# Adding the masked values of the two parities on VectorE before TensorE sums the heads, with a rewritten order of instructions

## The chip, the cores and the metric

The kernel runs on one core of a Trainium2 chip. The core has five engines, each with its own instruction queue: PE (TensorE, matrix multiplication, with a separate queue entry PEld for loading the stationary operand), DVE (VectorE), ACT (ScalarE), POOL (GpSimd) and SP (SyncE, which here only issues DMA transfers). Matmuls write to PSUM, which has eight banks; everything else works on SBUF. The metric is the device time of one execution in microseconds, as the median of several. The kernel before takes 224.31 us (three runs, 224.06 to 224.98).

## The reference, cut to what matters

Two rows (t = 0 and 1) of 128 tokens with 512 channels pass three residual blocks: a self-attention with a cross-attention over 2048 context tokens and a feed-forward part, an RWKV block, and a "switch head" attention. The change lies in the last, and reorders all of them. The last block has 8 heads of 64 channels and 5 experts; each head chooses 2 of 5 experts for its values and 2 of 5 for its output:

```python
q = (x @ Wq).reshape(b, t, h, dh).transpose(0, 2, 1, 3)
k = (x @ Wk).reshape(b, t, h, dh).transpose(0, 2, 1, 3)
gl_v = (x @ Ws).reshape(b, t, h, e)
wv = _topk_mask(gl_v, SEL) * jax.nn.sigmoid(gl_v)
xv = jnp.einsum('btd,edk->btek', x, Wv)
v = jnp.einsum('bthe,btek->bhtk', wv, xv)
probs = jax.nn.softmax(jnp.einsum('bhid,bhjd->bhij', q * scale, k), axis=-1)
attn = jnp.einsum('bhij,bhjd->bihd', probs, v)
gl_o = (x @ Wd).reshape(b, t, h, e)
mask_o = _topk_mask(gl_o, SEL)
out = jnp.einsum('bthe,bthk,ekd->btd', mask_o, attn, Wo)
```

The last line is what the change touches: for every token, the attention output of a head (64 values) is multiplied by the 0/1 mask of its 5 experts, the products of the 8 heads are summed to 5 x 64 = 320 values, and these go through a 320 x 512 projection.

## The kernel before, in words

All work is written down first and issued afterwards. The calls on the engines are recorded in a list (`Engine`, L172 to L182), one entry per instruction, 1759 in all, and `Program.emit` (L166) issues them in the sequence that the string `ORDER` (L42 to L99) gives, a list of entry numbers written out by hand. The order of the instructions on every engine, SP's DMA queue included, follows from that string. Since all are issued from one line, nearly all rows of the profile carry L169, and the tiles' names tell them apart.

The phases are, for both rows: queries and self-attention, `cross_queries`, `cross_attention`, `feed_forward`, `rwkv`, `switch_heads`. In the order they overlap: while row 0 is in one phase, row 1 is in the same or the one before. Four resources tie them together:

- Weights for matrix products that run as two halves (high and low part, fp32r) are loaded in pieces of 128 x 512 into a tag of three buffers (`stage`, L330); ACT casts each piece to its high half and DVE subtracts to get the low half. A load on SP waits until the piece three before it has been subtracted, and holds all loads behind it in SP's queue. In the profile these are the casts and subtractions `hl_Wv<-w_Wv`, `hl_fc2`, `hl_Wk` and so on.
- Context pieces (1 MB; `cT` for the scores, `cN` for the values) are loaded into 16 buffers of 8 KB a partition (`wide`, L201), shared with whole weights such as fc1, Wa, Wg, Wf, and with `me` and `ve` in the last phase. They are cast and subtracted in the same manner (`hl_ctxT`, `hl_ctxN`).
- The eight banks of PSUM (`bank`, L198).
- Tiles of 128 x 512 (`row`, L207).

In the cross-attention the number of context tokens that count is found from the scores (`em`, `left`, a small matmul with `nones`, `nsb` on ACT, then `some` and the masked exponentials). In the feed-forward part fc1 gives `zf` and its halves `zTh`. In `rwkv`, DVE forms K, the norms and decay products (`kn`, `kk`, `pr`, `kkar`, `kr`, `rn`, `wd`), then `Y` for each row, which PE turns and multiplies by Wo; `spread` tiles hold parameter rows, among them LNFB, which is added to the residual `X` in place.

`switch_heads` (L999): `xn` is turned to `xnT`; `w_fcat` gives the gates and the experts' values, `w_fWq` and `w_fWk` give queries and keys. DVE finds the top two experts by comparing all pairs (`gt`, `eq`, `ahead`, `sel`), and `v` from five products `ve`. Heads are taken by parity: heads 0, 2, 4, 6 share one PSUM bank for the scores (`nb`, `es`, `eT` for the softmax) and one for the attention output, heads 1, 3, 5, 7 the others. `ri` is the reciprocal of the softmax's sums, `mo` the output mask times `ri`. For each parity, `me` holds 4 heads x 5 experts x 64 masked values.

The two rows end differently. Row 0 adds all its masked values on DVE and turns the sum. Row 1 leaves the sum over the heads to PE: a matmul of a 128-wide piece of `me` (two experts) with the identity matrix `unit` turns the piece and accumulates in PSUM, so that 8 matmuls (4 heads, 2 parities) give one of three 128-row chunks of the turned sum `aT`; ACT copies it out, and `w_fWo` is applied. The three chunks start at experts 0, 2 and 3; the third overlaps the second by one expert, whose rows in the third chunk of `w_fWo` are zero. For row 1 the second parity's products are made in pieces of two, two and one experts (`pairs`), the first parity's in one instruction.

`keep_warm` issues matmuls of `unit` with itself; four of them are given for the first chunk of row 1's end, and the order places them well before it.

Of the kernel before, what the change touches and what calls it, by code (L numbers as in the profile page):

```python
# [42 lines left out]
0 208 1 209+1 215 2 1698 216+1 1718 218 1719 219+1 1699 232 221 1700 8 4 211 3 212 233 222 25 234 20 235+1 214 213 238  # L43
237 228 223+1 26 239 229 21+1 31 244+1 225 246 1720 270 240 247 27 230+1 241 271+3 248 275+2 249 28 34 37 226 23+1
278+1 250+5 280 242 227 256 281 257 243 258+2 282+1 261+3 284+1 265+1 286 29 292 30 32 293+1 287+2 267 35 318 33 295+2
319+1 38 298 36 299+1 321 39 301 322 302+2 323+4 305 328+1 306+1 330+1 5 308+1 332 310+4 333+2 315 40+1 49 43+1 11 19
336 9 337+2 290 268+1 317 340+1 344+1 414 316 415 45 42 346+1 375 12 50 79 46+1 84 376 66 48 291 343 358+1 342 360 377
361 416 51 362 378 348 363 18 379 417 364 87 67 63 418 104 380 419 349 381 365 384 382 56 420 423 350+4 395 366 383
385+1 85 387+2 421+1 424 390 425 69 426 391 6 355 367+1 392 357 396 356 427 393 428 369 429 68 434 371 370 372 397 394
398+3 430 402 373 431+1 435 404+1 433 57 403 436+2 406 1721 407+3 1701 453 463 411 454 10 80 439 455 464 456 465 457  # L50
441 443 466 440 442 447 467 444 468 82 458+2 448 469 74 445 86 88 446 473 483 474 470 450 449 475+2 484+2 478+2 58 64
60+1 471 81 461 481 487+2 493 94 59 62 89 494 490 495+1 462 482 521+2 497 491 65 75 472 524 492 498 525+2 499 528 500
529 109 83 530 501+4 531 97 126 532 374 506 533 77 76 534 507+6 535+1 95 514+2 537+2 98 540 517 541+1 588+1 562 96 518
543+1 563 72 575 564 576 545 78 519 590+2 577 593 565+6 594 578 546 579 70 73 572 549 573 580+1 550 582+1 71 551+2 105
584+1 99 547 106 520 548 92+1 554 586 555+1 595 90 727 596 557 91 558+2 597+1 728 157 599 107 729 102 100 574 108 587
121 127 561 730+2 600 112 733+1 129 735 601+3 101 736+1 618 740+5 738 605 611 606 612 609 746+1 753 748+1 610 607+1
613 54 766+1 754+1 750+1 768+1 615 614 756+2 641 770 623+3 642 771 122 759 103 760 55 643 761 772 616 627 128 773+1
762 775+2 130 644 739 628 123 629 617 630+4 124 635 125 645 137 136 138 763+1 646 752 765 928 636 659 778 660+2 637
140 638+2 779 131 142 663+1 780 647+4 132+1 652+2 781 113+1 134 782 655+1 796 168 657+1 665+1 677 667 135 668 785 783
678 669+2 679 672 787 680 13 15 110 786 784 673+2 789 681 790 676 682+1 619 684 788 791 145 197 792 17 14 794 52 837+2  # L60
7 840 801+1 795 855 803 53 169 139 793 804+1 685 819+1 807 821 856 822 808 857 141 16 111 146 806 809+2 686 812+1 118
143 687 823 814 688 815 689 816+1 692 818 144 825+1 693 824 827+1 858 147 158+1 690 696 829 697 691 830 698+1 831 700
832+2 701 835 841+1 412 115+1 694 702 119 703 413 120 695 117 704+1 150 620 152 706 836 148+1 621 187 622 859 188 151
843+1 707 710 708 711 709 712 845+3 713 163+1 178 849+1 179 714 797 715 451 851+1 165 189 853+1 860+1 716 720+1 153
862 717 723 722 718 180 719 863 904 864 725 905+1 916 866 917 867 907+2 452 865 870+1 868 874 910 875+2 911 170 981
724 869 872 878 154 879 155 880+2 918 160 166 873 883+2 919 161 920+1 913 912 156 914 726 922+1 929+1 798+2 175 931
176 924 167 932 925 162 926 915 933 172 888 886 934+2 889 887 890+2 937 177 938 184 927 893 939+1 894+1 898 199 943
941 896+1 944 942 899+1 969 957 901 173 970 945 958+4 185 963+1 946 966 947+1 971+1 951 949 952 965 950 953+1 973+2
967 955 976+1 956 982 968 983+2 193 902 978 986 1010 987 1011 979 988 1013+1 989+1 1012 991 980 992 1015 1089 1016 993
1017 1099 174 186 181 903 994 1090 996 1020 1067 1022 1069 1108 1018 1107 997 995 998 1091 1024 1140 1092 1073 1109  # L70
1026 1071 1141+1 1139 1028 1100 1029 1075 1093+1 1076 198 1077 1095 1030+1 1101 1070 1021 190 1096 1023 1032 1078 999
182 1033 1102 1116+1 1068 1079 1034 1080 191 196 1001 1004 1000 1025 1005 1035 1002 1006 1003 1007 183 1008 1103 1027
1009 1036 171 1072 1218+1 1081 1037 1221 194 1038 1082 1220 1222 1224+1 1039 1223 1097 195 192 1111 1110 1228 1324
1083 1112+2 1118 1323 1327 1119 1226 1229 1325 1333 1328 1084 1334+1 1326 1085 1336 1045 1329 1040 1074 1086 1343 1231
1279 1098 1282 1307 1346 1330 1280 1308 1232 1281 1233 1283 1046 1305 1344 1230 1234 1044 1306 1115 1047 1284 1286+2
1042+1 1104 1285 1019 1289 1337 1290 1347 1291+1 1235 1293+1 1120 1105 1087 1041 1048 1352 1295 1088 1296 1345 1391
1353 1297 1354+1 1348 1148+1 1392 200 1054 1389 1349+1 1106 1390 1050+1 1309 1150+1 201 1052 1331 1049 1121 1123 1236
1055 1061 1338 1124 1393 1299 1298 1300 1053 1060 1125 1310 1332 1311+1 1237 1122 1356 1339 1127 1238+3 1131 1242+1
1058 1244+1 1301 1341 1059 1246+2 1143 1340 1056 1062 1132 1351 1144 1128 1064 1342 1133 1063 1065 1302 1129 1357 1130
1303 1399 1145+1 1135 1057 1126 1313 1066 1314 1152 1359 1315 1253 1136 1254 1360 1137 1376 1358 1400 1316+3 1256 1252  # L80
1249 204 1250 1170 1401 1134 1251 1255 1138 1153 1257 1264 1258+1 1377 1261 1154 1361 1265 1155 1304 1147 1156 1158+1
1263 1320 1157 1161+1 1164 202 1369 1262 1260 1268 1321 1160 1165 1171 1166 1163 1167 1172 1168 1363 1378 1173+1 1276
1402 1198 1190 1394 1322 1277 1395 207 1373 1278 1379 1273 1267 1270 1269 1374 1380 1382 1362 1272 1371 1375 1274 1169
1396 1364 1271 203 1366 1275 1175 1381 1176 1383 1177 1384 1372 1385+2 1365 1178 1367+1 1388 1180 1179 1370 1266
1181+2 1397 1184 1186 1185 1187+1 1199+2 1189 1202 1191+1 205 1193+1 1403 1398 1203 1404 1406 1405 1407+2 1204 1410+1
1205 1424 1415 1195 1412+2 1416 1418 1417 1419+2 1196+1 1206+3 1212 206 1210 1213 1211 1214+3 1473 1425 1452 1426+2
1422 1472 1475+1 1444 1474 1423 1478+1 1429+2 1477 1481 1480 1432 1487 1482 1434 1433 1436 1435 1227 1437 1483 1440+1
1484 1438+1 1442 1488 1445 1485 1446 1489 1522 1453+2 1523 1447 1443 1513 1456 1448 1511 1486 1457 1524+1 1505 1526+1
1514+1 1490 1516 1496+1 1491+1 1517 1528 1518 1529 1493+1 1498 1519 1499 1520 1506+4 1500 1449 1521 1495 1530 1501
1512 1531 1502+2 1559 1534 1458 1450 1459 1451 1460+3 1466 1464 1467 1465 1468+2 1533 1471 1560+2 1602 1601 1603 1532  # L90
1604 1607+1 1563 1605 1539+2 1606 1567 1542 1564 1536 1610 1609 1543 1565 1611 1566 1535 1612+1 1569 1545 1544 1547
1546 1570 1552 1642 1549 1643 1572+1 1550 1614 1571 1551 1651 1553+1 1652 1537+1 1653 1555 1575 1556 1576 1574 1577
1548 1616 1654 1557+1 1617 1635 1634 1636+1 1568 1644+1 1618+1 1578 1646+1 1620+1 1648 1615 1625 1655 1622 1656 1623
1649 1638 1657 1640 1582 1650 1658 1624 1626+4 1639 1631 1659 1632 1688+1 1633 1579 1641 1663+1 1580 1583 1581 1690+1
1584 1660 1585 1662 1668+2 1586 1692 1671 1696 1587 1661 1588+1 1695 1672 1590 1705 1676 1706 1596 1591 1597 1673+1
1678 1675 1681 1679 1682 1665 1694 1592 1666 1693 1702 1667 1703 1680 1684+1 1683 1686 1677 1712 1687 1707 1697 1704
1708 1713 1709+2 1714 1716+1 1715 1598 1593 1731+1 1722 1733 1740+1 1734 1594 1599 1735 1600 1742 1723+4 1736+1 1743
1728+1 1738 1744+1 1730 1749 1746 1739 1747+1 1595 1754 1750+3 1755+3
"""  # L99
OPT = set("""psc fc2 Wv Wk u2col bfpe z4pe z1pe q2 hhcol q2row d3 both1 both4""".split())  # L100

ON_ACT = [set("vsum vc vv bv".split()), set("vsum vc vv bv".split())]
PCR = [{0,1,2},{0,1,2}]
WHOLE = set("Wv1 Wv2 fc2 Wv Wk".split())
VPE = set()
MIX = {"Wq1": 2}
MIXD = set("Ww Wa Wr".split())
CUTW = 2
# [77 lines left out]
def perceiver_kernel(ctx: ExitStack, tc: tile.TileContext, a: dict, out: bass.AP):  # L186
# [46 lines left out]
    for t in range(T):  # L233
        for j in range(2):
            sync.dma_start(X[t][:, half(j)], a["x"][t][:, half(j)])
# [296 lines left out]
    def token(t):  # L532
        return slice(t * P, (t + 1) * P)
# [678 lines left out]
```

## Time and profile before

| What | us |
|---|---|
| median of three runs | 224.31 |
| profiled execution, whole | 224.74 |
| its span in the profile | 222.9 |
| PE busy | 215.3 (97%) |
| DVE busy | 186.1 (83%) |
| ACT busy | 140.2 (63%) |
| last matmuls of the gates for row 1 (`w_fcat`) start | 189.90 |
| first matmul of row 1 with `v` starts | 208.56 |
| first sum of row 1's masked values starts | 211.29 |
| last addition (`res`) starts | 219.47 |

A line of the timeline gives the start, the duration, the engine, the line, the operation, the tiles (result first), their shapes and the count of equal instructions in a row; in brackets stands how long the engine had been idle before it and what ended the wait. The granted clock of TensorE was 0.998 of full speed. A matrix product in plain f32 shows as two records for each matmul. PE's records overlap, so the distance between starts is the cost of one, and not its duration. The span is 1.8 us shorter than the whole profiled execution, which is 0.43 us above the median.

### The profile page before, as it was taken

To read this page: it belongs to the slowest core of one execution; us is meant where nothing else is said; L and a number is where in the kernel's file an instruction comes from. 1 tells how busy PE (TensorE), PEld (TensorE's weight loads), DVE (VectorE), ACT (ScalarE), POOL (GpSimd) and SP (SyncE) were. 2 spreads that over 40 slices of the span, in tenths; PEclk is the share of its full clock that TensorE was granted. 3 is DMA by queue.
4 is the path that set the end of the run, shared out by engine and by line. 5 is a ranking of instruction groups with operands and counts; after the bars stand their busy time and mean duration, and the time that the engine had idled before them with its cause. 6 is when DMAs were issued, how large, how long until landed. Compare 5 with 4: busy or idle time off the path is not lost.

```text
span 222.9 us, 3686 instructions
## 1 busy us (share of the span) xinstructions
PE 215.3 (97%) x1246; PEld 182.7 (82%) x1246; DVE 186.1 (83%) x439; ACT 140.2 (63%) x400; POOL 17.1 (8%) x40
## 2 busy tenths in 40 slices
PE   6999999999999999999999999999999999998993
PEld 6999879998778767868788888887886799797892
DVE  4670569998999998989989999999998598999831
ACT  2753569686788998827469889977652614705500
POOL 4200011000000000000111100021213001000000
PEclk9999999999999999999999999999999999999999
DMA  6987799926699999587854999900000000000011
GB/s 157 355 322 255 250 381 386 385 110 238 245 315 354 374 399 375 202 285 209 310 187 102 402 389 387 303 7 0 3 0 0 0 3 1 0 3 0 0 50 47
DMA packets 21897, 43.42 MB, mean 195 GB/s; under 512 B 1283, under 2 KB 2871, under 8 KB 21879
## 3 DMA queue, kind: packets, MB, share of 16 engines
q1 hardware_dynamic: 21879, 43.19, 55.1%
q8 instruction: 10, 0.16, 0.3%
q14 instruction: 8, 0.07, 0.1%
HBM read 42.66 MB, written 0.52 MB: 194 GB/s over the span
## 4 chain that ended last, share of the span: by engine, by line
PE 64%; DVE 24%; DMA 3%; issue 2%; POOL 2%; ACT 2%; SPq 0%; POOLq 0%; DVEq 0%
PE bank L169 64%; DMA w_Wv<-in_Wv_dram 3%; DVE me L169 2%; DVE hl_ctxT L169 2%; DVE Y L169 2%; DVE pr L169 2%; DVE st L169 1%; DVE em L169 1%; DVE hl_ctxN L169 1%; POOL rinv L169 1%; POOL rs L169 1%; DVE ve L169 1%; DVE v L169 1%; DVE u L169 1%; DVE hl_Wv L169 1%
## 5 line engine op out<-in xcount | busy, mean ns | idle before, releaser
L169 POOL TENSOR_TENSOR rinv<-ve,nhalf 128x1 f32<-128x1 f32 x16 | 10.1, 629 | 147.2 <-DVE ve L169 75.4
L169 DVE TENSOR_TENSOR hl_ctxT<-cT,hl_ctxT 128x1024 fp32r<-128x1024 f32 x16 | 19.0, 1216 | 0.8 <-ACT hl_ctxT L169 0.5
L169 PE MATMUL bank<-hl_ctxT,qkTh 128*128 128x512 f32 x64 | 17.8, 395 | 0.1
L169 ACT CAST hl_ctxT<-cT 128x1024 fp32r<-128x1024 f32 x16 | 16.0, 1050 | 2.5 <-PE bank L169 2.5
L169 PE MATMUL bank<-hl_ctxN,pTh 128*128 128x512 f32 x48 | 16.3, 402 | 0.0
L169 DVE TENSOR_TENSOR hl_ctxN<-cN,hl_ctxN 128x1024 fp32r<-128x1024 f32 x12 | 14.4, 1217 | 0.6 <-ACT hl_ctxN L169 0.6
L169 PEld LDWEIGHTS bank<-hl_ctxT,qkTh 128*128 128x128 f32 x64 | 11.7, 188 | 2.8 <-DVE some L169 0.5
L169 DVE TENSOR_TENSOR hl_Wv<-w_Wv,hl_Wv 128x512 fp32r<-128x512 f32 x12 | 8.0, 681 | 6.4 <-ACT hl_Wv L169 6.4
L169 ACT CAST hl_ctxN<-cN 128x1024 fp32r<-128x1024 f32 x12 | 12.3, 1046 | 0.0
L169 PE MATMUL bank<-hl_ctxT,qkTl 128*128 128x512 f32 x32 | 10.4, 396 | 0.0
L169 PEld LDWEIGHTS bank<-hl_ctxN,pTh 128*128 128x128 f32 x48 | 8.9, 189 | 1.6
L169 PE MATMUL bank<-xnT,w_fWk 128*128 128x128 f32 x64 | 10.2, 276 | 0.0
L169 PE MATMUL bank<-hl_ctxN,pTl 128*128 128x512 f32 x24 | 10.1, 421 | 0.0
L169 ACT CAST hl_Wv<-w_Wv 128x512 fp32r<-128x512 f32 x12 | 7.3, 622 | 4.0 <-DMA w_Wv<-in_Wv_dram 3.9
L169 PE MATMUL bank<-xnT,w_fWq 128*128 128x128 f32 x64 | 9.9, 277 | 0.0
L169 PEld LDWEIGHTS bank<-u2T,w_fc 128*128 128x128 f32 x64 | 8.2, 191 | 1.4 <-ACT u2T L169 1.1
L169 PEld LDWEIGHTS bank<-xnT,w_fWq 128*128 128x128 f32 x64 | 8.6, 192 | 0.7 <-ACT xnT L169 0.3
L169 PEld LDWEIGHTS bank<-xnT,w_fWk 128*128 128x128 f32 x64 | 8.9, 192 | 0.2
L169 PE MATMUL bank<-u2T,w_fc 128*128 128x128 f32 x64 | 8.5, 278 | 0.3 <-ACT u2T L169 0.3
L169 PE MATMUL bank<-w_Wa,mix 128*128 128x256 f32 x32 | 8.7, 379 | 0.0
L169 PE MATMUL bank<-unit 128*128 128x128 f32 x32 | 6.9, 391 | 1.7 <-POOL unit masks.py:199 1.7
L169 PE MATMUL bank<-w_Wr,mix 128*128 128x256 f32 x32 | 8.4, 379 | 0.0
(289 smaller groups left out, 614.8 us busy)
## 6 DMA issues: line engine op xcount, KB each, us to landing
cT<-in_ctxT_dram SPq DMA_DIRECT2D x8, 1024.0 KB, 6.7
cN<-in_ctx_dram SPq DMA_DIRECT2D x8, 1024.0 KB, 7.5
spread<-in_spread_dram SPq DMA_DIRECT2D x9, 512.0 KB, 8.5
w_Wv<-in_Wv_dram SPq DMA_DIRECT2D x12, 256.0 KB, 5.3
w_Wk<-in_Wk_dram SPq DMA_DIRECT2D x8, 256.0 KB, 5.3
w_Wq<-in_Wq_dram SPq DMA_DIRECT2D x4, 256.0 KB, 4.5
w_Wk2T<-in_Wk2T_dram SPq DMA_DIRECT2D x4, 256.0 KB, 6.9
w_Wq<-in_Wq_dram SPq DMA_DIRECT2D x1, 1024.0 KB
```

Of the source, the lines that this page charges most:

```text
L169: self.tc.keep_in_program_order(op(*args, **kwargs))
```

## The change

In `switch_heads`, for row 1 and before the sums of each chunk, DVE adds the second parity's masked values to the first's, for the experts of that chunk's pair (two, two, one). The chunk is then summed by four matmuls, not eight. In numbers of recorded calls: three DVE additions more (4 heads x 2, 2 and 1 experts x 64), twelve f32 matmuls of 128 x 128 fewer. Loads, ACT's and POOL's work are the same sets as before.

`ORDER` is rewritten as a whole: 1750 instructions of the changed program in a new sequence on all engines, SP's loads included. The diff also adds code for options that are not switched on (`xact`, `pow1`, `u1back`), and takes out an unused one (`veps`); none of these changes an instruction.

```diff
-OPT = set("""psc fc2 Wv Wk u2col bfpe z4pe z1pe q2 hhcol q2row d3 both1 both4""".split())
+OPT = set("""psc me2 fc2 Wv Wk u2col bfpe z4pe z1pe q2 hhcol q2row d3 both1 both4""".split())
...
             for c, e in enumerate((0, 2, 3)):
                 pt = bank([P, P])
                 keep_warm(0 if c else TAILW[2], pt)
-                matmuls(pt, [(m[:, i, e : e + 2, :].rearrange("p e d -> p (e d)"), unit) for m in me for i in range(4)], True)
+                if "me2" in OPT:
+                    n = pairs[c]
+                    dve.tensor_add(me[0][:, :, n], me[0][:, :, n], me[1][:, :, n])
+                ms = me[:1] if "me2" in OPT else me
+                matmuls(pt, [(m[:, i, e : e + 2, :].rearrange("p e d -> p (e d)"), unit) for m in ms for i in range(4)], True)
                 act.copy(aT[:, c, :], pt)
```

Parts of the new order that the prediction speaks of, told by what is issued on each engine:

- End of row 1, DVE: both reciprocals and both `mo`, the odd parity's products of the pairs 2-3 and 0-1, the even parity's product, the additions for 2-3 and 0-1, the odd product of the last expert, the last addition. Before: the even product first, then the three odd ones. PE: the odd parity's matmuls with `v` first, then all six matmuls of row 0's `w_fWo`, the twelve sums (chunks at 2, 0, 3), six matmuls of row 1's `w_fWo`. Before, four of row 0's six stood ahead of the matmuls with `v`, and one of row 1's six between the sums.
- `rwkv`: the addition of LNFB to row 1's X, the reduction `kkar` and the first half of `wd` that stood behind row 0's Y now stand ahead of it; the reduction `kr` of row 1 and `rn` now stand behind.
- Feed-forward: no cast of a weight stands between ACT's `zf` activations of row 0.
- Loads on SP: a `cT` piece ahead of two pieces of Wv1; one piece of Wv2 right behind the pieces of Wk2T; the first `cN` piece behind three `cT` pieces; fc1 behind a second fc2 piece and a pair of `spread` rows; Wa behind fc1; fWk, Wr, Wo, Wg, Ww in this sequence; Wf last.
- POOL: the iota for `kidx` after two of the first reciprocal roots; the clearing of `w_fWo`'s last rows ahead of most of the later roots.

## The prediction

> **What bounds the kernel now.** I read the page's busy times and slices first, then the chain of work that ended last, then the waits of the tensor engine (PE), then the timeline of the stages that the change touches. The page and the chain:
>
> ```profile
> span 222.9 us, 3686 instructions
> PE 215.3 (97%) x1246; PEld 182.7 (82%) x1246; DVE 186.1 (83%) x439; ACT 140.2 (63%) x400; POOL 17.1 (8%) x40
> PE 64%; DVE 24%; DMA 3%; issue 2%; POOL 2%; ACT 2%; SPq 0%; POOLq 0%; DVEq 0%
> ```
>
> PE has an instruction in flight nearly always, but the chain gives PE only 64%: in between it runs over the vector engine (DVE). Which of the two ends last differs by stage. The waits view, for PE:
>
> ```profile
> PE bank L169 <- POOL unit masks.py:199: 1.7, 1, 1.7
> PE bank L169 <- ACT es L169: 0.7, 1, 0.7
> PE bank L169 <- DVE left L169: 0.4, 1, 0.4
> PE bank L169 <- ACT zTh L169: 0.3, 1, 0.3
> ```
>
> Beyond the first 1.7 us PE's gaps are few; with those too short for this view I add them up to about 5 us over the span. So removed PE work pays one for one only if what PE waits for afterwards is not later. The end of the kernel, from the timeline (start, duration, what):
>
> ```profile
> 207.72 0.69 DVE L169 TENSOR_TENSOR v<-v,ve 128x512 f32<-128x512 f32 x1
> 208.56 1.97 PE L169 MATMUL bank<-v,eT 128*128 128x64 f32 x16
> 209.67 1.49 DVE L169 TENSOR_TENSOR me<-bank,mo 128x1280 f32<-128x1280 f32 x1 [0.87 <-PE bank L169]
> 211.29 5.11 PE L169 MATMUL bank<-unit,me 128*128 128x128 f32 x44
> 211.34 1.62 DVE L169 TENSOR_TENSOR me<-bank,mo 128x512 f32<-128x512 f32 x3
> 216.24 0.60 PE L169 MATMUL bank<-w_fWo,aT 128*128 128x256 f32 x2
> 217.11 2.32 PE L169 MATMUL bank<-w_fWo,aT 128*128 128x256 f32 x10
> 219.47 0.42 DVE L169 TENSOR_TENSOR res<-bank,X 128x256 f32<-128x256 f32 x1 [0.44 <-PE bank L169]
> ```
>
> The reader is to see a handover: until 211.2 DVE's masked products hold PE back, from 211.29 to the end PE alone is late and DVE is idle from 213.6 to 218.6.
>
> **The price of the tail edit.** Removed: 12 of the 24 sums of masked values. Each is two records; 44 records start within 5.11 - 0.28 us, so 0.112 apart, 0.223 a matmul, 12 x 0.223 = 2.68 us. Added: three DVE additions of 512, 512 and 256 elements a partition. The three products at 211.34 have these sizes, and the next instruction starts 1.54 later: 0.61 + 0.61 + 0.33; an addition that depends on its forerunner costs its full 0.69. No trace row prices a 256-wide addition in SBUF; the 320-wide one holds DVE 0.45, the 256-wide product 0.33, and either does.
>
> Now the path. Where DVE computed row 1's v, one reciprocal and one mo of row 0 (0.21 together) have gone ahead, so v ends at 208.20 for 208.41; the matmuls with it start 0.15 later, as before, at 208.35, and their order has changed: the odd parity's bank comes first. Its first product can start 1.11 behind, at 209.46. Then DVE does two odd products (0.61 each) to 210.68, the even 1280-wide one (1.49) to 212.17, and only then the first addition, ready at about 212.9. The first sum starts at 212.97, not 211.29: the new wait costs 1.68. Behind it in PE's queue stand only the sums and row 1's output projection; the wait is partly filled, since all six of row 0's projection matmuls (0.432 each, 2.59) now stand after v's, where four ran ahead before. They end by 212.7 and cost nothing themselves. From 212.97: 12 x 0.223 to 215.65, then six projection matmuls, 2.59, to 218.24. Before, five stood behind the last sum at 217.11 and ended at 219.27. **The tail gives 1.03 us**, not 2.68. The second and third addition end at 213.5 and 214.3, ahead of PE's need at 213.86 and 214.75. Bounds: 2.68 if the additions were free, nothing if the odd products and additions came 1 us later still.
>
> [...]
>
> **The rest of the order.** PE's work ahead of the tail is the same set of matmuls, phase by phase in the same sequence to 1-2 us. What moves are casts, loads and some DVE work.
>
> (a) At 110.5 a stall goes. The scalar engine (ACT) took a weight cast, late by its load, ahead of the activations that PE needs:
>
> ```profile
> 108.88 0.62 ACT L169 CAST hl_Wv<-w_Wv 128x512 fp32r<-128x512 f32 x1 [2.12 <-DMA w_Wv<-in_Wv_dram]
> 109.41 0.62 ACT L169 ACTIVATE zf<-bank,cols 128x128 f32<-128x128 f32 x2
> 110.52 1.20 PE L169 MATMUL bank<-hl_fc,zTh 128*128 128x512 f32 x4 [0.34 <-ACT zTh L169]
> ```
>
> In the new order no weight cast stands between these activations: -0.5 (the cast's 0.53 hold). Next late would be the second u2T, 0.33 at 112.9, untouched. Against it: a piece of fc2 is cast just ahead; were its load late, +0.6. I take -0.5.
>
> (b) DVE from 126 to 172 has almost no idle time, and the chain runs over it from 143 on. Ahead of row 0's Y go the LNFB addition to X1 (0.60; it filled an idle place at 174.45 before), a reduction kkar (0.60) and half of wd (0.33); kr (0.60) and rn (0.19) go behind: +0.74. Before, DVE idled 0.33 for PE and 0.35 for POOL's power there:
>
> ```profile
> 143.61 0.69 DVE L169 TENSOR_TENSOR pr<-kn,kk 128x512 f32<-128x512 f32 x1 [0.33 <-PE bank L169]
> 151.38 0.17 DVE L169 TENSOR_TENSOR c<-kr,rs 128x8 f32<-128x8 f32 x1 [0.35 <-POOL rs L169]
> ```
>
> Both gaps lie behind moved work and can take 0.68 of it. I take +0.1; bounds 0 and +0.74.
>
> (c) From 20 to 34, ACT and DVE do about 3.5 us more context casts ahead of u1T, since one 1 MB context load goes ahead of two weight pieces. The slices show 30 to 60% idle there on both. One subtraction of 1.14 stands ahead of row 1's normalization. I take +0.2; bounds 0 and +1.1.
>
> (d) From 54 to 62, DVE's work ahead of left is equal to 0.1, but PE reaches left's matmul 0.45 of work earlier: +0.1; bounds -0.2 and +0.45.
>
> (e) SP's queue: the loads of fc1, of Wa, Wg, Ww and Wf and of the context pieces change places. I took for each the instruction it waits for, in the new order's places, against its first use. fc1's (1 MB, first used at 101.75) now stands behind a fc2 piece and a 0.5 MB row load, issued at about 94.2 for 95.13: even 7 us, more than its 6.1 before, lands in time. Wf goes last, behind a wait at 135.4, used at 164. POOL's iota and a clearing of w_fWo move to places where POOL idles (8% busy). All at nothing; cover gone, the price of a late load is one for one (rival 2).
>
> Sum: -1.03 - 0.5 + 0.1 + 0.2 + 0.1 = -1.13. The profiled execution took 224.74 us (span 222.9 and 1.8 around it); the median of the runs is 224.31. I take the sum off the median: **223.2**, 0.5% below. About 0.5%, 1.1 us, is also what a measurement of this kernel can tell from no change.
>
> **Rivals.** *1. Half of PE's sums are simply gone.* If DVE's products and additions end before PE gets there, all 2.68 come: 224.31 - 2.68 - 0.1 (the rest of the order) = 221.5. For it: DVE idles from 213.6. Against it: that idleness comes too late, the first sum needs three products and an addition in a row. 0.10.
>
> *2. Slower, by a context load.* The first cN piece was issued at 40.8; in the new order it waits for a bank_287 matmul that PE reaches at about 51.8. ACT must cast it (2 x 0.95) ahead of the mask value that releases row 0's softmax, nsb at 61.4. So it decides at a landing of 59.45, that is 7.65 us after issue; the median of the eight such loads is 7.5. Each us beyond holds PE one us, since row 1's scores behind wait for banks that the softmax frees; beyond 9.9 us the kernel is slower by over 0.5%. With 3 MB in flight I estimate 10.5 (3.1 MB at the 0.39 MB a us of the busiest slices, and 2.4 as the smallest loads take): PE loses 2.8 and the time is 223.2 + 2.8 = 226.0. Against it: the slices from 50 to 61 us show the DMA engines at 6 tenths, so some 1 to 2 MB in flight. 0.23.
>
> *3. The order eats the gain.* The bounds of (b), (c) and (d) at their dear ends, 0.74 + 0.4 + 0.45 with (a) kept, leave 224.31 - 1.03 - 0.5 + 1.59 = 224.4: no change. 0.25.
>
> The forecast itself, 222.6 to 223.8, has 0.42. Faster by over 0.5% (below 223.2): 0.32 of the forecast's and rival 1's 0.10. Slower (above 225.4): 0.21 of rival 2 and 0.04 of rival 3. The rest, 0.33, is within 0.5%. To hold 8 in 10 the range leaves out most of rival 1 and the far half of rival 2: 222.0 to 225.6. Cases of both signs hold much of the chance; the forecast's own range is 222.6 to 223.8.
>
> **What would show it.** The tail: the first sum 4.6 us after the first matmul with v (2.73 before), at once behind the first addition; 24 records of sums, not 48; the last result 25.5 us after the gates' matmuls end at 192.9 (26.6 before). (a) is right if PE's wait for zTh is gone. (b) is wrong if Y's transposes at 154 come 0.5 later against the start of their phase. Rival 2 shows as PE waiting about 62 for some or em with ACT waiting for cN. I am wrong if a load that I called covered holds ACT, which no sum of durations can exclude.

## The result, and the profile after

The changed kernel takes **227.34 us** (median of four runs, 226.14 to 227.60) beside 224.47 for the kernel before (224.06 to 224.98): ratio 1.0109, 95% interval 1.0079 to 1.0139. It is slower by 1.1%; 223.2 was forecast, with an upper end of 225.6. The profiled execution took 227.6 us, 2.3 of them outside its span of 225.3; in the execution before, 1.8 lay outside. Counted from the span's start, the last result begins 5.4 and 5.3 us before the whole time is over, so starts within the two spans can be compared directly. Ratios leave out executions more than 1.5% above the fastest of the same kernel (433.63 and 758.71 us in two later runs; 228.49, 226.97, 226.56 and 227.13 us in the table further down), and medians count them.

From the page of the changed kernel; the third line is the clock that TensorE was granted, in tenths, over 40 slices of 5.6 us (before, all 40 show 9):

```profile
span 225.3 us, 3636 instructions
PE 216.8 (96%) x1222; PEld 182.5 (81%) x1222; DVE 188.6 (84%) x442; ACT 140.3 (62%) x400; POOL 17.1 (8%) x40
...
PEclk9999999999999999999999999999999999997579
...
PE 65%; DVE 17%; DMA 9%; ACT 4%; POOL 2%; issue 1%; SPq 1%; DVEq 0%; POOLq 0%; ACTq 0%
```

PE is busy for longer (216.8 for 215.3 us) with 24 records fewer. Its matmuls got slower, and the clock row says where: in slices 37 to 39, the tail. The same in finer stretches (length, PE's busy time and its records, granted clock, DMA share, GB/s):

```profile
204.00:206.00 2.00, 0.94 (x8) 1.00 0.00 0
206.00:207.00 1.00, 0.60 (x3) 0.54 0.00 0
207.00:212.00 5.00, 5.00 (x25) 0.50 0.00 0
212.00:216.00 4.00, 4.00 (x11) 0.50 0.00 0
216.00:217.00 1.00, 1.00 (x7) 0.84 0.00 0
217.00:222.00 5.00, 5.00 (x36) 1.00 0.17 56
```

From about 206.1 to 216.3 us PE ran at half its clock. Ahead of that, between 204 and 206, it was busy for 0.94 of 2 us; before, for 1.32, and the clock stayed at 1.00:

```profile
204.00:206.00 2.00, 1.32 (x10) 1.00 0.00 0
```

In the changed kernel, PE's waits name the two holes (0.8 for `me`, 0.6 for `es`):

```profile
PE bank L166 <- POOL nhalf L166: 1.7, 1, 1.7
PE bank L166 <- DVE me L166: 0.8, 1, 0.8
PE bank L166 <- ACT es L166: 0.6, 1, 0.6
PE bank L166 <- ACT pT L166: 0.6, 1, 0.6
...
PE bank L166 <- DMA w_fc<-in_fc_dram: 0.4, 1, 0.4
```

The wait for `zTh` is gone, as forecast; a wait for `pT` and one for fc1's load stand there that the profile of before doesn't have. The tail itself, from the timeline of PE and DVE:

```profile
205.35 0.41 PE L166 MATMUL bank<-ident,me 128*128 128x128 f32 x2 [0.81 <-DVE me L166]
206.40 1.17 PE L166 MATMUL bank<-ident,es 128*128 128x128 f32 x4 [0.64 <-ACT es L166]
...
208.66 3.51 PE L166 MATMUL bank<-v,eT 128*128 128x64 f32 x16
210.50 1.29 DVE L166 TENSOR_TENSOR me<-bank,mo 128x512 f32<-128x512 f32 x2 [1.65 <-PE bank L166]
211.97 4.96 PE L166 MATMUL bank<-w_fWo,aT 128*128 128x256 f32 x12
216.77 2.84 PE L166 MATMUL bank<-unit,me 128*128 128x128 f32 x24
219.44 2.75 PE L166 MATMUL bank<-w_fWo,aT 128*128 128x256 f32 x12
222.24 0.42 DVE L166 TENSOR_TENSOR res<-bank,X 128x256 f32<-128x256 f32 x1 [0.44 <-PE bank L166]
```

The matmuls with `v` start at 208.66, where they did before (208.56): until there the new order is neutral in this execution. They take 3.51 us where they took 1.97, and row 0's six projection matmuls 4.96 for a summed 2.6. The first sum starts 8.11 us after the first matmul with `v` (before 2.73, forecast 4.62). From the first sum on the edit saves what it should: 5.47 us to the last result, 8.18 before. Together 5.38 lost and 2.71 won: 2.77 us with the 0.10 at the start, of the 2.86 between the two executions.

### The profile page after: what moved, and what is told of

Its sections match the earlier page's. It is cut to its first block, busy times and chain, and to the rows that moved or that the text cites. A ratio compares the mean times of both kernels' runs of the same rounds, so it can differ in the third digit from the quotient of the medians.

```text
span 225.3 us, 3636 instructions
## 1 busy us (share of the span) xinstructions
PE 216.8 (96%) x1222; PEld 182.5 (81%) x1222; DVE 188.6 (84%) x442; ACT 140.3 (62%) x400; POOL 17.1 (8%) x40
## 4 chain that ended last, share of the span: by engine, by line
PE 65%; DVE 17%; DMA 9%; ACT 4%; POOL 2%; issue 1%; SPq 1%; DVEq 0%; POOLq 0%; ACTq 0%
PE bank L166 65%; DMA w_fc<-in_fc_dram 4%; DMA cN<-in_ctx_dram 3%; DVE Y L166 2%; DVE hl_ctxN L166 2%; ACT em L166 2%; DVE pr L166 2%; DVE me L166 2%; DMA X<-in_x_dram 1%; DVE ve L166 1%; POOL rinv L166 1%; POOL rs L166 1%; DVE v L166 1%; ACT es L166 1%; DVE hl_ctxT L166 1%
## 5 line engine op out<-in xcount | busy, mean ns | idle before, releaser
L166 POOL TENSOR_TENSOR rinv<-ve,nhalf 128x1 f32<-128x1 f32 x16 | 10.3, 646 | 146.0 <-DVE ve L166 137.3
L166 PE MATMUL bank<-hl_ctxT,qkTh 128*128 128x512 f32 x64 | 18.3, 398 | 0.0
L166 PE MATMUL bank<-hl_ctxT,qkTl 128*128 128x512 f32 x32 | 10.9, 393 | 0.0
L166 PE MATMUL bank<-xnT,w_fWk 128*128 128x128 f32 x64 | 9.6, 277 | 0.0
L166 PEld LDWEIGHTS bank<-xnT,w_fWk 128*128 128x128 f32 x64 | 8.4, 192 | 0.1
L166 PE MATMUL bank<-w_Wg,mix 128*128 128x256 f32 x32 | 8.4, 379 | 0.0
L166 DVE TENSOR_SCALAR_CACHE_REDUCE em<-bank 1x512 f32<-1x512 f32 (+1 forms) x10 | 5.8, 594 | 3.0 <-PE bank L166 3.0
L166 PE MATMUL bank<-w_Wa,mix 128*128 128x256 f32 x32 | 8.2, 379 | 0.0
```

Source lines behind the costliest of these rows:

```text
L166: self.tc.keep_in_program_order(op(*args, **kwargs))
```

## The experiments

**Theory C (clock):** the new order takes four projection matmuls of row 0 out of the stretch where PE waits for DVE and ACT, behind the matmuls with `v`; PE idles there, its clock is halved, and the tail runs at half speed. **Theory W (waits):** the waits and the later projection cost the time as they stand, and the clock is a by-product.

### Filler matmuls in both holes

Seven matmuls of `unit` with itself, 0.223 us each, into banks that nobody reads yet: four ahead of the turn of row 0's `me`, three ahead of a turn of `es`. The diff shows the code and the order's text.

```diff
             pt = bank([P, 3, P])
+            st["fill"] = [pt[:, 0, :]]
...
                 pt = bank([P, 2, P])
+                if t and j and not par:
+                    st["fill"].append(pt[:, 0, :])
...
+    with program.on("fill"):
+        for o, n in zip(st["fill"], (4, 3)):
+            keep_warm(n, o)
     program.emit(ORDER)
...
-1586+2 1672 1675 1681
+1586 1750+3 1587+1 1672 1675 1754+2 1681
```

> The changed kernel with seven more matmuls of the identity with itself, put where PE idles at 204.5 to 206.4 (four ahead of row 0's turns, three ahead of the first es turn); nothing else moves. Clock theory (the idle time makes the granted clock fall to 0.5 for 10 us): the clock stays at 1.0 to the end and the tail ends 3.5 us earlier, 227.3 - 3.5 = 223.8 us (223.0 to 224.6). Wait theory (the additions and the projection matmuls moved behind v hold PE, the low clock only fills the waits): no change, 226.8 to 227.8.

Measured: 224.2 us (ten runs, 222.87 to 225.38), ratio to before 0.9975 (0.995 to 0.9999). More PE work makes the kernel 3.1 us faster than the changed one. The clock was 1.0 throughout, and the tail is the one that the prediction summed:

```profile
189.75 2.95 PE L168 MATMUL bank<-w_fcat,xnT 128*128 128x400 f32 x8
...
208.03 2.10 PE L168 MATMUL bank<-v,eT 128*128 128x64 f32 x16
209.18 2.69 DVE L168 TENSOR_TENSOR me<-bank,mo 128x512 f32<-128x512 f32 x3 [0.75 <-PE bank L168]
209.97 2.81 PE L168 MATMUL bank<-w_fWo,aT 128*128 128x256 f32 x12
...
212.73 2.92 PE L168 MATMUL bank<-unit,me 128*128 128x128 f32 x24
215.49 2.76 PE L168 MATMUL bank<-w_fWo,aT 128*128 128x256 f32 x12
218.28 0.42 DVE L168 TENSOR_TENSOR res<-bank,X 128x256 f32<-128x256 f32 x1 [0.44 <-PE bank L168]
```

First product 1.15 us behind the first matmul with `v` (1.11 in the prediction), first sum 4.70 (4.62), last result 5.55 behind that. It comes 1.19 earlier than before, 0.15 of which was won ahead of the gates of row 1: from their last matmuls to the last result it takes 28.53 us (189.75 to 218.28), for 29.57 before, 1.04 less. Row 0's projection fills the wait for DVE. Theory W falls: its 226.8 is missed by far.

### The same projection moved in the kernel before, without the edit

Row 0's four projection matmuls go behind those with `v`; nothing else changes.

```diff
-1676 1706 1596 1591 1597 1673+1
+1676 1706 1673+1
...
-1694 1592 1666
+1694 1666
...
-1715 1598 1593
+1715 1596 1591 1597 1592 1598 1593
```

> The kernel before, without the edit, with row 0's four projection matmuls moved from among the es turns to behind the matmuls with v, as the new order has them. Clock theory: the clock falls to 0.5 at about 206 to 209 for 7 to 10 us, 227 to 229. Wait theory: the moved matmuls cost their 1.73 us, 226.1, with the clock at 1.0. Neither: 224.4.

Measured: 229.58 us (228.38 to 230.74), ratio 1.0208 (1.0162 to 1.0255); the mean granted clock was 0.978 to 0.985 in all four runs, and in the profile 0.50 from 207 to 217. This move alone, without any addition, is enough for the drop.

### The same, with filler near the old places

Eight fillers (1.78 us) near where the four projection matmuls (1.73 us) had been. Six of them stand one turn of `es` later than the first three matmuls did, behind PE's second wait for `es`.

```diff
+                if t and j + par == 1:
+                    st.setdefault("fill", []).append(pt[:, 0, :])
...
+    with program.on("fill"):
+        for o, n in zip(st["fill"], (6, 2)):
+            keep_warm(n, o)
     program.emit(ORDER)
...
-1673+1 1678 1675 1681
+1673+1 1678 1675 1759+5 1681
...
-1693 1702
+1693 1765+1 1702
```

> The kernel before with row 0's four projection matmuls moved behind those with v, as in the run without the fill, and eight filler matmuls (0.223 us each, 1.78 together) in their old places: PE has the same work before row 1's values as before and 1.73 us more behind them. Theory, that the 5.1 us of the run without the fill were 1.7 of later projection and 3.3 of a lower clock: 226.2 us (225.7 to 226.8), granted clock 1.0. Rival, that the lateness of the projection alone, or the waits, cost the 5.1: 229.5.

Measured: 227.15 us (226.45 to 227.59), ratio 1.0099 (1.0066 to 1.0132), mean clock 1.0 in three runs and 0.992 in one. Of the 5.0 us that the move cost, 2.4 went with the clock and 2.6 stayed. Both terms are real, in other shares than expected (3.3 and 1.7). In the profiled execution (226.45) the stretch from the first matmul with `v` to the last result grew by 1.62 us (208.63 to 221.16, for 208.56 to 219.47), near the 1.73 of the moved work; the rest of the 2.6 lies between that execution and the median, and isn't assigned. One thing in this profile speaks against a simple reading of theory C. PE's two waits ahead of the fillers are as long as in the run without them (0.69 and 0.76 us), and between 204 and 206 PE is busy for less than in the changed kernel, yet the clock holds (a stretch as above, then the timeline):

```profile
204.00:206.00 2.00, 0.68 (x5) 1.00 0.00 0
206.13 0.33 PE L170 MATMUL bank<-ident,es 128*128 128x128 f32 x1 [0.76 <-ACT es L170]
206.30 1.50 PE L170 MATMUL bank<-unit 128*128 128x128 f32 x12
```

So idle time up to that point doesn't decide alone. Without the fillers the clock fell in four executions of four, with them in one of four.

### The edit alone, in the order before

```diff
-1714 1716+1 1715 1598 1593
+1714 1716 1728 1715 1722 1717 1734 1598 1593 1729+3 1723+3 1735+3
```

The additions 1728, 1722 and 1734 stand right behind the products that they need; row 0's projection stays ahead.

> The kernel before with the edit alone: three additions, twelve sums fewer, and the tail's order of before. By rows: first sum 212.5 for 211.29, 12 x 0.223 fewer, -1.1: 223.3 us (222.8 to 224.0) if the clock holds. If the edit itself is what costs, or its wait lowers the clock: 225 or more.

Measured: 224.0 us, ratio 0.9956 (0.9933 to 0.9978), by the ratio 1.0 us faster. The profile shows where most of the rest of the 2.7 us went:

```profile
208.42 1.97 PE L170 MATMUL bank<-v,eT 128*128 128x64 f32 x16
210.22 1.08 PE L170 MATMUL bank<-w_fWo,aT 128*128 128x256 f32 x4
212.76 3.29 PE L170 MATMUL bank<-unit,me 128*128 128x128 f32 x24 [1.46 <-DVE me L170]
215.88 2.76 PE L170 MATMUL bank<-w_fWo,aT 128*128 128x256 f32 x12
```

PE waits 1.46 us for the first addition, so that the first sum comes 4.34 us behind the first matmul with `v`, for 2.73 before. The clock still holds at 1.00. So a hole of that length does not always lower it, and the edit was never the loss: the order was.

### The changed order up to row 1's scores, then the tail of before with the edit

```diff
-1630+1 1624 1632 1688 1638+1 1689 1633 1583
+1630+1 1624 1632 1638+1 1688+1 1633 1641 1663+1
...
```

The dots stand for the rest of the order: from there on it is before's order of the same instructions, with the additions placed as in the run above.

> The changed kernel up to row 1's scores, from there the order of before with the three additions put in: four of row 0's six projection matmuls are again ahead of the matmuls with v. Clock theory: PE has work in the gap, the clock stays at 1.0, 223.2 to 224.2. Wait theory: only the 1.7 us of moved projection comes back, about 225.6. If the additions' wait of some 1.2 us at 211.3 is itself enough to lower the clock: 225 to 226.5 with the clock at 0.5 from 212 on.

A miss: 227.09 us (226.4 to 229.41), ratio 1.0116 (1.0058 to 1.0174), mean clock 0.984 to 1.0. One execution held the clock (1.0) and still took 226.4 us, which the clock doesn't explain. In the profile DVE waits 1.45 us for PE ahead of row 0's two products, which start at 198.79 us, for 197.29 before; so `me` comes later than in either kernel:

```profile
205.63 0.52 PE L167 MATMUL bank<-ident,me 128*128 128x128 f32 x3 [1.39 <-DVE me L167]
206.98 0.69 PE L167 MATMUL bank<-ident,es 128*128 128x128 f32 x2 [0.83 <-ACT es L167]
207.46 2.81 PE L167 MATMUL bank<-w_fWo,aT 128*128 128x256 f32 x6
```

The projection matmuls are back, but stand behind the holes, and the clock has already fallen (from 206.1 on 0.50): 2.81 us for six records that took 1.56. Behind holes this long, the work came too late to hold the clock; behind the shorter ones of the run with eight fillers it helped.

### How much filler, and of what kind

The next runs are the changed kernel with less or other filler. The order's text changes at the same two places.

```diff
-        for o, n in zip(st["fill"], (4, 3)):
+        for o, n in zip(st["fill"], (4, 0)):
```

(4, 0) fills the first hole alone, (0, 3) the second, (2, 0) and (1, 0) a part of the first.

> The changed kernel with the four filler matmuls of the first hole alone (PE idle 0.97 us there in the changed kernel); the second hole (0.70) stays open. Theory A, that the idle time of the last few us adds up and the clock falls only somewhere above the 1.6 us that the old order with the edit bore at full clock: some 0.9 us is left, the clock stays at 1.0, 224.2 us (223.6 to 224.8). Rival B, that every hole of this place must be filled: the clock falls and the time is 227.3.

> The changed kernel with the three filler matmuls of the second hole alone; the first hole, 0.97 us, stays open. Theory A: about 1.1 us idle is left, the clock stays at 1.0, 224.2 us (223.6 to 225). Rival B (every hole), or a rival C by which the longest hole counts: the clock falls to a half again, 227.3.

> The same with two filler matmuls (0.45 us): about 1.4 us idle is left, as much as the old order with the edit bore in one piece at full clock. By the sum of idle time full clock in all executions, 224.0 us (223.4 to 224.6); if that order bore it for another reason (its wait stands behind busy work, here two holes follow one another), the clock still falls in some: 225.5 to 227.

> The changed kernel with one filler matmul of 0.22 us in the first hole: about 1.6 us idle of 1.8 is left before the place where the clock fell. If the sum of idle time decides and lies between 1.4 (full clock) and 1.8 (half), this is near the edge: some executions at half clock (227), some at full (224). If any PE work in the first hole is enough: all at full clock, 224.

Two more tell idle time from kind of work: eight turns of `unit` in the first hole in place of four matmuls, and row 0's three turns of `me` as plain matmuls, with no filler.

```diff
+    with program.on("fill"):
+        for _ in range(8):
+            pe.transpose(st["fill"][0], unit, ident)
     program.emit(ORDER)
```

```diff
-                pe.transpose(pt[:, c, :], at[:, e * HD : e * HD + P], ident)
+                matmuls(pt[:, c, :], [(at[:, e * HD : e * HD + P], unit)], True)
```

> The changed kernel with eight transposes of unit (0.11 us each, 0.9 together) in the first hole, where the run with four filler matmuls (0.223 each, 0.9 together) held the clock in nine executions of nine. Theory I, that the idle time decides: 0.9 us idle is left as there, full clock in all, 224.0 us (223.4 to 224.6). Theory M, that transposes do not count as work for the clock, so that the stretch from the last scores to the first matmul with v, 4.1 us in the changed kernel, stays empty of ordinary matmuls: the clock falls in nearly all, 227 us (226.3 to 227.8).

> The changed kernel with row 0's three transposes of me written as matmuls with unit (0.223 us each for 0.11), where they stand: two between the holes, one among the transposes of es. The first hole stays (0.97 us), the second shrinks by 0.2: 1.6 us idle, as in the run with one filler matmul, where the clock fell in at least six of nine. Theory I (idle time): it falls in most, 226.5 us (225.8 to 227.3). Theory M (transposes do not count): the stretch without ordinary matmuls is cut into 0.9, 1.5 and 1.2 us, full clock in all, 224.2 us (223.6 to 224.8).

Measured; "fallen" are executions with a mean clock of 0.992 or less, "idle" is the sum of PE's idle times in brackets in the profile between the last scores and the matmuls with `v`, "stretch" the longest time there without an ordinary matmul (turns and idle time only):

| Kernel | idle, us | stretch, us | fallen | median, us | ratio to before |
|---|---|---|---|---|---|
| changed kernel | 1.45 | 4.1 | 4 of 4 | 227.34 | 1.0109 (1.0079 to 1.0139) |
| one filler | 1.54 | 3.5 | 6 of 9 | 226.55 | 1.0059 (1.0025 to 1.0093) |
| turns of `me` as matmuls | 1.60 | 1.2 | 3 of 9 | 224.37 | 0.9992 (0.9952 to 1.0031) |
| eight turns in the first hole | 0.96 | 3.9 | 2 of 9 | 224.27 | 0.9987 (0.995 to 1.0025) |
| two fillers | 1.24 | 3.3 | 1 of 9 | 224.2 | 0.9983 (0.9958 to 1.0008) |
| second hole filled | 1.35 | 2.0 | 0 of 9 | 223.97 | 0.9966 (0.9945 to 0.9987) |
| first hole filled | 1.10 | 2.8 | 0 of 9 | 223.8 | 0.9956 (0.9933 to 0.998) |
| both filled | 0.54 | 1.9 | 0 of 10 | 224.2 | 0.9975 (0.995 to 0.9999) |

With eight turns a ninth execution, the profiled one, had 0.95 over its whole span and no drop in the tail; it isn't counted as fallen. Nor is every long execution a fallen one: with one filler, one with a clock of 1.0 took 226.75 us. The idle time of the changed kernel is not on a par with the rest: its clock fell before the last waits, and its slower turns cover those; with the waits of 0.15 and 0.39 that four other rows' profiles show there, it would be about 2.0, an estimate. The run with eight fillers in the order before, by the same count, has 1.45 us idle, a stretch of 2.5 and 1 of 4 fallen. The profiled execution with one filler shows the drop at 209.0, at the end of four us in which PE was busy for 2.45:

```profile
205.00:206.00 1.00, 0.69 (x5) 1.00 0.00 0
206.00:207.00 1.00, 0.30 (x3) 1.00 0.00 0
207.00:208.00 1.00, 0.85 (x6) 1.00 0.00 0
208.00:209.00 1.00, 0.61 (x6) 1.00 0.00 0
209.00:210.00 1.00, 1.00 (x6) 0.52 0.00 0
...
214.00:216.00 2.00, 2.00 (x7) 0.53 0.00 0
216.00:218.00 2.00, 2.00 (x16) 1.00 0.00 0
```

What follows: either hole filled is enough, 0.45 us of filler nearly is, 0.22 is not. This dose series shows theory C by degrees. What exactly is counted stays open. If idle time alone decided, eight turns would have held the clock in all and the turns as matmuls would have lost it in most; if only ordinary matmuls counted, eight turns would have lost it in nearly all and the turns as matmuls held it in all. Both came out in between, so theories I and M both fall in their pure form. The same kernel falls in some executions and not in others, so near the edge it differs from one execution to the next; what decides it there isn't shown.

The Trainium skill's page "TensorE: Matmul & The Clock Gate", section "What's actually happening", says that the clock goes to half after an idle window of about 3.4 us, and that this window runs freely. The runs differ on the first: the waits ahead of the drop were of 0.15 to 1.4 us, and PE was busy for 0.94 of the 2 us and 2.45 of the 4 us before it in the two stretches above; the second would fit that the same kernel falls in six executions of nine, but no run here shows a window.

### The load of fc1

On top of the seven fillers, fc1's load goes ahead of the pair of `spread` rows.

```diff
-157+1 160+1 168 797
+157+1 160+1 153 168 797
...
-722+1 153 916
+722+1 916
```

> The changed kernel with all seven filler matmuls (clock held, 224.2 us), and on SP's queue the load of fc1 ahead of the pair of spread rows that was issued just before it. Theory, that these 0.5 MB stand in fc1's way: 1.3 us of transfers less ahead of it and 0.4 us earlier, it lands about 1.5 us earlier, PE's wait for it (0.4 in that run, 0.5 in the changed kernel) goes: 223.8 us (223.2 to 224.4). Rival, that the load is long whatever stands ahead, since other queued loads follow at once: wait and time stay.

Measured: 224.09 us (222.91 to 225.0), ratio 0.9988 (0.9968 to 1.0009). In the profile PE's wait for fc1 is gone. Of nine profiles of the new order with the pair ahead, eight show that wait (0.3 to 1.5 us) and one doesn't, so this fits a pair that stood in the way; a single profile doesn't prove it. In time the 0.1 us against 224.2 can't be told from nothing.

### Versions made from the order before

The edit for the first and third chunk; the second, which needs the fewest products, keeps its eight matmuls and goes first. The code is shown against the changed kernel, the order against the one before.

```diff
-                if "me2" in OPT:
+                if "me2" in OPT and c != 1:
...
-                ms = me[:1] if "me2" in OPT else me
+                ms = me[:1] if "me2" in OPT and c != 1 else me
...
-1714 1716+1 1715 1598 1593
+1714 1716 1715 1722 1717 1737 1598 1593 1728+7 1594 1599+1 1736 1723+4 1738+4
```

> The order of before, with the edit for the first and the third chunk only: the second chunk (experts 2 and 3) keeps its eight matmuls and no addition, and is summed first, since it needs only the even product and one odd one. DVE adds 0-1 and 4 behind. PE starts its sums at 211.3 as before, not behind an addition: 16 sums of 0.223 in place of 24 (-1.78), about 0.15 us of waiting for the first addition: 224.4 - 1.6 = 222.8 us (222.3 to 223.3), granted clock 1.0. Rival, that the waits for DVE take the gain as they took 1.7 of 2.7 in the full edit: 223.8 or more.

Measured: 223.56 us (222.3 to 224.65), ratio 0.9948 (0.9921 to 0.9974): about 1 us faster than before, above the 222.3 to 223.3 us that were expected, and not clearly better than the full edit in that order (0.9956). In the tail the mechanism holds, with no wait ahead of the sums:

```profile
209.54 1.97 PE L170 MATMUL bank<-v,eT 128*128 128x64 f32 x16
211.35 1.08 PE L170 MATMUL bank<-w_fWo,aT 128*128 128x256 f32 x4
212.27 4.18 PE L170 MATMUL bank<-unit,me 128*128 128x128 f32 x32
216.28 2.76 PE L170 MATMUL bank<-w_fWo,aT 128*128 128x256 f32 x12
```

The first sum comes 2.73 us behind the first matmul with `v`, as before, and the last result 9.55 us behind it for 10.91: 1.36 won of the 1.63 expected. This execution lost 1.21 us on `zTh`, the stall of (a), because the piece of Wv came later:

```profile
109.86 0.62 ACT L170 CAST hl_Wv<-w_Wv 128x512 fp32r<-128x512 f32 x1 [3.00 <-DMA w_Wv<-in_Wv_dram]
```

So that cast was moved behind the activations, in a last run:

```diff
-175 931 176 924
+175 931 924
...
-162 926 915
+162 926 176 915
```

> The order of before with the edit for the first and third chunk, as in the run before, and ACT's cast of the late piece of Wv put behind the activations of row 0's feed-forward that PE waits for, the one stall that the new order removed as the prediction said. PE's wait for zTh (0.3 us in the profile of before, 1.2 in that of the run without this move, where the load came later) goes: 0.5 to 1.2 us below the 223.6 of that run: 222.9 us (222.3 to 223.4). Rival, that the cast is then late for its own products or that the next late one, u2T, takes the gain: 223.6.

Measured: 223.77 us, ratio 0.997 (0.9952 to 0.9987). No gain over the run without it. Its profile is of the execution of 758.71 us and doesn't show whether the wait went. So the best versions found stand about half a percent below before.

## Why the prediction was wrong

**The tail: the step that failed.** "They end by 212.7 and cost nothing themselves", of row 0's six projection matmuls behind v's. The first half holds while the clock does (in the run with fillers they end at 212.78, where the first sum starts at 212.73). But four of them had been the work between row 1's scores and the matmuls with `v`; I asked what they would cost in their new place and not what their old place was left with. There PE had turns and waits alone, and its granted clock fell to 0.50 for 10.2 us. Measured price: 227.34 against 223.8 to 224.2 in the runs that held the clock, 3.1 to 3.5 us. The slices of before showed the holes (PE's 0.68 us ahead of the turns of `es`) and a clock of 9 tenths everywhere; no row of it shows a drop, so no sum of its rows had this term.

**The gain of the tail, 1.03 us.** Right with the clock held: from the gates' last matmuls to the last result it is 1.04 in the profiled execution with fillers, and four more profiles with that end and the clock at 1.00 have the same 28.53 us (29.57 before). The last result then stands 25.58 us behind the gates' end, as the prediction asked (25.5). The later first sum, 1.68 by the prediction, is 1.6 behind the first matmul with `v` for the edit alone in the old order (4.34 for 2.73), of which PE waits 1.46.

**(a), the stall at 110.5.** Right: PE's wait for `zTh` is gone, in ten profiles with the new feed-forward. Its size is not fixed: five profiles of the old one have 0, 0, 0.3, 0.9 and 1.2 us, so -0.5 was no fixed size.

**(b), (c), (d).** The early part came out better than I took it: the matmul of `left` for row 0 starts 0.98 us earlier than before (I had summed +0.3), since neither dear end came true. Y's turn in `rwkv` starts 0.33 later (154.47 for 154.14), when the stages before it were level (+0.02 at the feed-forward's end): more than the +0.1, within the bounds and short of the 0.5 that would have made (b) wrong.

**(e), loads at nothing.** Wrong twice. The chain of the changed kernel holds two transfers in the middle:

```profile
71.20 7.29 DMA cN<-in_ctx_dram
...
78.52 1.05 ACT hl_ctxN L166
79.57 1.24 ACT em L166 x2
80.80 0.48 ACT pT L166
...
93.21 9.15 DMA w_fc<-in_fc_dram
...
102.50 1.57 PE bank L166 x12
```

fc1's load was issued at 93.2, before the 94.2 of the prediction, but was under way for 9.15 us, not 7, with the pair of rows beside it: 0.4 us of PE. (Nine profiles of the new order with the pair ahead have 8.6 to 10.3 us for this load, five of the old order 5.6 to 7.3.) A `cN` piece held ACT's cast, `em` and `pT` behind it, and with them PE for 0.6 at 81.3. These two used up the early gain: the gates of row 1 end 0.26 us later than before, where (a) to (d) sum to -0.1. This early part isn't fixed either: in the five profiles with 28.53 us behind it, the gates' last matmuls start 0.23 us earlier to 1.32 us later than before, and the latest has the longest wait for fc1 (1.5 us). With the clock held the kernel is only 0.4 to 0.8 us faster than before in the medians, not 1.13.

**The rivals.** Rival 1 (all 2.68 us) is out: with the clock held the first sum comes 4.34 and 4.70 us behind the first matmul with `v` in the two orders, for 2.73 before. Rival 2 named the right side and the wrong place: nothing was late for `nsb` at 62; its mechanism, ACT waiting for a context piece, cost 0.6 at 81 and decided nothing. Rival 3 (the order eats the gain) describes the kernel with the clock held best, but by loads, not by the ends of (b) to (d). None contained what decided.

## What to carry to other kernels

When work moves out of a stretch where an engine waits, ask first what the stretch is left with, and look at the granted clock there: here the moved matmuls were worth more as cover (2.4 us, by the run with eight fillers) than their own 1.73 us. A short matmul on data that nobody reads, put into the hole, costs nothing where PE would idle and showed here within one run whether the clock was the cause. A load's time from issue to landing in the old order (6.1 us for fc1) is no measure of it in the new one (9.15), where other loads are issued just ahead of it.

## What the runs showed of the hardware

The granted clock fell after waits of 0.15 to 1.4 us each, with PE idle for about 1.1 to 1.6 us of the four before. A wait of 1.46 us between busy stretches left it alone (edit in the old order, clock 0.997 or more in all runs), and so did waits of 0.69 and 0.76 us with fillers behind them (three executions of four). Once it fell it stayed at 0.50 for about 6.9 us (one filler, 209.0 to 215.9) or 10.2 us (changed kernel), though PE was busy without a break but for the first 0.3 us. The mean clocks of 0.992, 0.985 and 0.977 that fallen executions have work out to 3.6, 6.7 and 10.3 us at half (one minus the mean, doubled, times 224 us), an estimate that takes the rest of the span at 1.0. Plain f32 matmuls at half clock took 3.51 for 1.97 us (16 records with `v`) and 4.96 for 2.76 (12 records of the projection).
